# Another order of the scan directions, a layer norm finished half by half, and routing arithmetic with operands in PSUM

## The chip, the cores and the metric

The kernel runs as one program on one core of a Trainium2 chip. The metric is the device time of one execution in microseconds (us). Three timed executions of the kernel before took 4451.01, 4462.27 and 4446.85 us; their median is 4451.01 us. The profiled execution is a fourth one.

The core has five engines with a queue each, and each queue runs in order: TensorE (PE in the profile, its weight loads PEld), VectorE (DVE), ScalarE (ACT), GpSimd (POOL) and SyncE (SP), which here issues most of the transfers. SBUF and PSUM are the two on-chip memories; PSUM has eight banks of 128 x 512 fp32 values.

## The reference, cut to what matters

Four images of 384 channels x 32 x 32 pass through two layers. All is fp32.

```python
# layer 0
x = x + scan_conv(ln_channels(x, 1e-6))      # four scan directions, then layer norm and gelu
t = tokens(x)                                # [4, 1024, 384]
t = t + moe(ln_tokens(t, 1e-5))              # 4 experts, the best 2 of each token
# layer 1
x = x + attention(ln_channels(x, 1e-6))      # 8 heads over 1024 tokens
t = t + ffn(ln_tokens(t, 1e-5))              # weights are Kronecker products

def scan_conv(x):
    xs = [x, x.T, reversed(x), reversed(x.T)]        # k = 0..3: by rows, by columns, both again reversed
    for k: h = h * exp(dt * A) + dt * u * B;  y_k = sum_n(h * C) + u
    y = y_0 + y_2 + transpose back(y_1 + y_3)
    return gelu(ln_channels(y, 1e-5) * lnw + lnb)

def moe(t):
    p = softmax(t @ gate_w + gate_b); keep the two largest of four, divide by their sum + 1e-9
    return sum over the kept experts e of p_e * (gelu(t @ w1[e] + b1[e]) @ w2[e] + b2[e])
```

The sum of the four directions does not depend on the order in which they are added, apart from rounding.

## The kernel before, in words

**The scan** (`scan_layer`, lines 196 to 303). A *unit* is one image b, one direction k and one half i of the 1024 tokens (512 positions); the list `units` at lines 252 to 257 has 32 of them, eight to an image, in the order k = 0, 1, 2, 3. Directions 2 and 3 run backwards, so their second half comes first. Each unit has three channel chunks; `chunk` (line 401) makes for each of four groups g of states the products `bx` on POOL (L432, 128x1024), the decay `da` on ACT (L441, into PSUM), the recurrence on DVE (L446) and the product with C, half of it on POOL (L460) and half on DVE (L453). PE adds the states up into one PSUM bank `acc` (L467), and DVE adds `acc` to the output y (L294, L298). There are six buffers for `bx`, two for each group g, and each comes free when PE has read it at L467. In PSUM the scan has four banks: two for `da` and two under the tag "ps", which `acc`, the projections (`xd_ps`, `dt_ps`) and the layer norms (`ln_mean`, `ln_var`, `ln_rows`) share.

Beside a unit, `project` (line 305) prepares the next one. In the last unit of an image, `start` (line 223) loads the next image and norms both its halves first. After the last unit of an image `finish` (line 236) norms y (both halves, one after the other), applies gelu per chunk, adds the input on POOL (L247) and stores the result in DRAM as `x1[b]` (L248); then the tail of the image before it is emitted.

**The tail** of an image: `route` (line 611) with `spread` (line 616), which transposes the tokens of `x1[b]`, two blocks of 128 at a time, and computes gate scores; `places` (line 676), a chain of some 55 small DVE instructions that turns scores into row numbers, weights and expert numbers; then 16 indirect DMAs on POOL that scatter normed tokens into rows by expert (L664). `experts` (line 817) runs eleven slots of rows, `combine` (line 916) gathers the results, `prologue` (line 953) norms, `attention` (line 974) and `last_layers` (line 1077) follow. `less_mean` (line 540) is one DVE instruction of 128x8 used by `spread` and, through `prologue` and L958, by the attention: the ACT work at L960 waits for it. `divide` (line 1026) inverts the softmax sums (L1028).

**What sets the order.** A scheduler orders the instructions of each engine ahead of time from their program order (earlier is preferred), priorities (`high_priority` around `route`, `combine`, `prologue` and `last_layers`) and its own estimate of time. So the tail of image b-1 and the routing of image b run between the scan instructions of image b+1, in a fixed order per engine. During the scan the tail has four PSUM banks: two under the tag "s" (one tile), one "o" (expert outputs `y_ps`, attention `o_acc`, `f_acc` of the last layer) and one "p" (most else). When the scan is over, the tail of image 3 gets rooms of its own in what the scan leaves.

Of the kernel before, what the change touches and what calls it, by code (L numbers as in the profile page):

```python
# [9 lines left out]
F32 = mybir.dt.float32  # L10
# [16 lines left out]
KG = 4  # L27
NS = 16
# [86 lines left out]
class Body:  # L115
# [80 lines left out]
    def scan_layer(self, x1, between):  # L196

        nc, tc, a = self.nc, self.tc, self.a
        with ExitStack() as ctx:
# [36 lines left out]
            def finish(b, y):  # L236
                self.layernorm(y, y, self.eps5, psum, work)
                for c in range(DC):
                    ins = nc.scalar.activation(
                        y[:, c, :], y[:, c, :], AF.Gelu,  # L240
                        bias=self.col("lnb", c), scale=self.col("lnw", c),
                    ).ins
                    rows = slice(c * P, (c + 1) * P)
                    for i in range(NH):
                        x = work.tile([P, HF], F32, tag="k2", name="x", bufs=6)
                        nc.sync.dma_start(out=x, in_=a["x"][b][rows, halves(i)])
                        nc.gpsimd.tensor_add(x, x, y[:, c, halves(i)])  # L247
                        nc.sync.dma_start(out=x1[b][rows, halves(i)], in_=x)  # L248
                self.exp_again(ins)

# [4 lines left out]
                for k in range(KG)  # L255
# [10 lines left out]
            for n, unit in enumerate(units):  # L266
                b, k, i = unit
                fed, ahead = ahead, []
                project = iter(())
                if n + 1 < len(units):  # L270
                    nb = units[n + 1][0]
                    if nb not in us:
                        us[nb] = start(nb)
                    project = self.project(units[n + 1], us[nb], wx, work, dram, psum, ahead)
                    next(project)
                if n % NH == 0:
                    carry = wp.tile([P, NB * NG], F32, tag=f"carry{n // NH % 2}", name="carry")
                if k == 0 and i == 0:
                    y = work.tile([P, DC, L], F32, tag="y", name="y")
                for c in range(DC):  # L280
                    acc = psum.tile([P, HF], F32, tag="ps", name="acc")
                    for _ in self.chunk(
                        unit, n % NH == 0, c, fed, carry, nega, sel, acc, work, dap
                    ):
                        next(project, None)
                    if k % 2 == 0:
                        ys = y[:, c, halves(i)]
                        out = acc
                    else:
                        w = slice(i * (HW // NH), (i + 1) * (HW // NH))  # L290
                        ys = y[:, c, :].rearrange("p (h w) -> p h w", h=HW)[:, :, w]
                        out = acc.rearrange("p (w h) -> p h w", h=HW)
                    if k == 0:
                        nc.vector.scalar_tensor_tensor(  # L294
                            ys, us[b][:, c, halves(i)], dsum[:, c : c + 1], out, op0=ALU.mult, op1=ALU.add
                        )
                    else:
                        nc.vector.tensor_add(ys, ys, out)  # L298
                if k == KG - 1 and b not in self.under_way:
                    self.under_way[b] = fed[2]  # L300
                if n + 1 == len(units) or units[n + 1][0] != b:
                    finish(b, y)
                    between(b)
# [236 lines left out]
    def less_mean(self, mean, rstd, room, tag):  # L540

        less = room.tile([P, MB], tag, "less")
        self.nc.vector.scalar_tensor_tensor(less, mean, -1.0, rstd, op0=ALU.mult, op1=ALU.mult)
        return less
# [71 lines left out]
    def spread(self, b, x1, room):  # L616
# [10 lines left out]
        for m in range(0, MB, 2):  # L627
            x = room.tile([P, DC, 2 * P], "k4", "x")
            nc.sync.dma_start(out=x, in_=src[:, :, m * P : (m + 2) * P])
            xt = room.tile([P, 2, D], "k4", "xt")  # L630
            for o in range(2):
                ps = room.bank("p", "tt_ps")
                cols = slice(o * P, (o + 1) * P)
                for c in range(DC):
                    nc.tensor.transpose(ps[:, c * P : (c + 1) * P], x[:, c, cols], self.ident)
                for c in range(DC):
                    nc.tensor.matmul(
                        ps[:, D : D + NE], x[:, c, cols], self.wg[:, c, :],
                        start=(c == 0), stop=(c == DC - 1),
                    )  # L640
                nc.scalar.copy(xt[:, o, :], ps[:, :D])
                nc.vector.tensor_copy(sc[:, m + o, :], ps[:, D : D + NE])
                nc.vector.bn_stats(st[:, m + o, :], xt[:, o, :])
                nc.vector.bn_aggr(mv[:, m + o, :], st[:, m + o, :])
# [31 lines left out]
    def places(self, sc, room):  # L676
# [4 lines left out]

        def over(v):
            return v.unsqueeze(2).to_broadcast([P, nt, NE])

        red = room.tile([P, nt], "g_red", "g_red")
# [4 lines left out]
        nc.vector.reciprocal(red, red)  # L690
        nc.vector.tensor_mul(sc, sc, over(red))
# [3 lines left out]
        other = sc.unsqueeze(2).to_broadcast(shape)  # L695
        above = room.tile(shape, "g_above", "g_above")
        same = room.tile(shape, "g_same", "g_same")
# [5 lines left out]
        nc.vector.tensor_reduce(rank, above, AX.X, ALU.add)  # L703
        chosen = room.tile([P, TOP, nt, NE], "g_chosen", "g_chosen")
        for k in range(TOP):
            nc.vector.tensor_scalar(chosen[:, k], rank, float(k), None, op0=ALU.is_equal)
        nc.vector.tensor_scalar(rank, rank, float(TOP), None, op0=ALU.is_lt)
        nc.vector.tensor_mul(sc, sc, rank)
        nc.vector.tensor_reduce(red, sc, AX.X, ALU.add)
        nc.vector.tensor_scalar_add(red, red, 1e-9)  # L710
        nc.vector.reciprocal(red, red)
        nc.vector.tensor_mul(sc, sc, over(red))
# [7 lines left out]
        cnt = room.tile([P, 2, nt, NE], "g_cnt", "g_cnt")  # L720
        nc.vector.tensor_copy(cnt.rearrange("p t m e -> p (t m e)"), ps[:, : 2 * n])
        run = room.tile([P, nt + 1, NE], "g_run", "g_run")
        nc.vector.memset(run[:, 0, :], 0.0)
        for m in range(nt):
            nc.vector.tensor_add(run[:, m + 1, :], run[:, m, :], cnt[:, 1, m, :])

# [3 lines left out]
            need, run[:, nt, :].unsqueeze(2).to_broadcast([P, NE, ns]),  # L730
# [3 lines left out]
        used = room.tile([P, 2, NE], "g_used", "g_used")  # L734
        nc.vector.tensor_reduce(used[:, 1], need, AX.X, ALU.add)
        nc.vector.tensor_reduce(used[:, 0], need[:, :, 1::2], AX.X, ALU.add)
        nc.vector.scalar_tensor_tensor(
            used[:, 1], used[:, 0], -2.0, used[:, 1], op0=ALU.mult, op1=ALU.add
# [12 lines left out]
        shift = room.tile([P, 2, NE], "g_shift", "g_shift")  # L751
        full, back = shift[:, 0], shift[:, 1]
# [24 lines left out]
        nc.vector.tensor_add(at, at, ends)  # L777
        pick = room.tile([P, 2, TOP, nt, NE], "g_pick", "g_pick")
        both = [P, TOP, nt, NE]
        nc.vector.tensor_mul(pick[:, 0], chosen, at.unsqueeze(1).to_broadcast(both))  # L780
        nc.vector.tensor_mul(pick[:, 1], chosen, sc.unsqueeze(1).to_broadcast(both))
        picked = room.tile([P, 2, TOP, nt], "g_picked", "g_picked")
# [32 lines left out]
        return pos, picked[:, 1], expert  # L815
# [158 lines left out]
    def attention(self, xc, sums, room):  # L974
# [51 lines left out]
        def divide(t, att):  # L1026
            inv = room.tile([P, 2 * MB], "inv", "inv")
            nc.vector.tensor_add(inv, sums[:, t, :, 0], sums[:, t, :, 1])  # L1028
# [387 lines left out]
```

## Time and profile before

| quantity | value |
|---|---|
| three timed executions | 4451.01, 4462.27, 4446.85 us, median 4451.01 us |
| profiled execution, its own time | 4452.07 us |
| its span (first to last instruction) | 4450.2 us, so 1.9 us lie around it |
| mean granted TensorE clock | 0.850 |
| units of image 0 (from the first `bx` of one to that of the next) | 83.1 to 95.8 us |
| shortest and longest unit of images 1 to 3 | 97.5 us and 147.1 us |
| first `bx` product of images 0, 1, 2, 3 | at 47.8, 748.8, 1668.6, 2631.6 us |
| last addition of `acc` to y (end of the scan) | at 3569.1 us |
| first transpose of image 3's experts | at 3691.6 us |

How to read it: a timeline line has the start and the length in us, engine, line of the kernel, operation, out<-in, and how many instructions are merged; in brackets stands how long the engine was idle before, and what ended that. A group line has count, busy us and mean ns of one instruction, then the idle time before the group. A line of the 40 slices has one digit for each fortieth of the span (111 us): the busy share in tenths.

### The profile page before, as it was taken

The numbers are of one execution on the slowest core, as the hardware profiler recorded it, in microseconds if no ns is written. First come the engines' busy times: TensorE is split into PE (matmuls) and PEld (weight loads), VectorE is DVE, ScalarE is ACT, GpSimd is POOL, SyncE is SP. The second block draws the span as 40 slices with busy tenths as digits, with TensorE's granted clock in tenths as the row PEclk, the third lists the DMA queues.
The fourth block names the chain that finished last, engine by engine and source line by source line (L and its number), as shares of the span: only waits on it lengthen the run. The fifth ranks groups of instructions, "written<-read, shape, count | busy, mean of one in ns | idle before, by whom it ended". The sixth has DMA issues, their size and how long they took to land. (4 is left out here: it accounts for less than half of the span.)

```text
span 4450.2 us, 47090 instructions
## 1 busy us (share of the span) xinstructions
PE 3462.1 (78%) x13980; PEld 1644.5 (37%) x13980; DVE 2980.1 (67%) x4252; ACT 2469.7 (55%) x4380; POOL 3050.0 (69%) x1475
## 2 busy tenths in 40 slices
PE   6545554579995887669998688758998699999897
PEld 2111111245552222325555222214555334566333
DVE  5889998778887876978787777988787720020002
ACT  4545554456664766466666477466666453325354
POOL 4999999689988877779888689879888710000100
PEclk7766665579997998679999899869999899999898
DMA  4444453468785533357779434446778534344300
GB/s 121 119 124 114 129 162 91 134 225 233 217 253 169 164 93 116 117 174 217 209 229 274 134 99 120 123 145 193 215 212 261 171 106 139 123 135 164 102 17 15
DMA packets 404760, 684.81 MB, mean 154 GB/s; under 512 B 50960, under 2 KB 206480, under 8 KB 404496
## 3 DMA queue, kind: packets, MB, share of 16 engines
q1 hardware_dynamic: 395184, 655.37, 50.0%
q0 software_dynamic: 8192, 25.17, 1.7%
q8 instruction: 112, 1.84, 0.2%
q14 instruction: 152, 1.25, 0.1%
q10 hardware_dynamic: 1120, 1.18, 0.1%
HBM read 561.47 MB, written 120.06 MB: 153 GB/s over the span
## 5 line engine op out<-in xcount | busy, mean ns | idle before, releaser
L432 POOL TENSOR_TENSOR bx<-dtr,bcs 128x1024 f32<-128x1024 f32 x768 | 1793.5, 2362 | 211.5 <-PE acc L467 118.2
L441 ACT ACTIVATE da<-dtr,nega 128x512 f32<-128x512 f32 x1536 | 1045.8, 691 | 1013.9 <-DVE bx L453 637.7
L460 POOL TENSOR_TENSOR bx<-bx,bcs 128x1024 f32<-128x1024 f32 x384 | 904.0, 2360 | 216.9 <-DVE bx L446 94.9
L467 PE MATMUL acc<-bx,sel 128*32 128x512 f32 x3072 | 518.6, 712 | 304.2 <-POOL bx L460 258.4
L889 PE MATMUL h_ps<-xc,w 128*128 128x256 f32 (+1 forms) x3168 | 665.2, 364 | 43.6 <-DVE xc L871 21.1
L905 PE MATMUL y_ps<-w,hs 128*128 128x384 f32 x1824 | 644.1, 505 | 44.3 <-ACT hs L898 40.3
L889 PEld LDWEIGHTS h_ps<-xc,w 128*128 128x128 f32 x3168 | 547.4, 196 | 228.6 <-issue 92.0
L446 DVE TENSOR_TENSOR_SCAN bx<-da,carry,bx 128x512 f32<-128x512 f32 x384 | 473.9, 1269 | 125.1 <-ACT da L441 61.9
L446 DVE TENSOR_TENSOR_SCAN da<-da,carry,bx 128x512 f32<-128x512 f32 x384 | 477.3, 1273 | 70.6 <-ACT da L441 61.3
L446 DVE TENSOR_TENSOR_SCAN bx<-da,bx 128x512 f32<-128x512 f32 x384 | 451.8, 1209 | 102.6 <-POOL bx L432 61.3
L453 DVE TENSOR_TENSOR bx<-da,bcs 128x512 f32<-128x512 f32 x768 | 511.3, 680 | 4.5
L446 DVE TENSOR_TENSOR_SCAN da<-da,bx 128x512 f32<-128x512 f32 x384 | 455.7, 1219 | 74.5 <-ACT da L441 62.9
L905 PEld LDWEIGHTS y_ps<-w,hs 128*128 128x128 f32 x1824 | 348.6, 196 | 339.6 <-issue 78.2
L1020 ACT ACTIVATE ex<-s_ps 128x512 f32<-128x512 f32 x512 | 299.2, 590 | 207.1 <-PE s_ps L1015 206.1
L1015 PE MATMUL s_ps<-w 64*128 64x512 f32 x1024 | 307.6, 675 | 83.0 <-ACT ex L1020 83.0
L467 PEld LDWEIGHTS acc<-bx,sel 128*32 128x32 f32 x3072 | 78.6, 116 | 606.1 <-POOL bx L460 371.0
L1064 PE MATMUL o_acc<-ex,vt 128*64 128x512 f32 x1024 | 295.3, 657 | 0.6 <-ACT att L1072 0.5
L894 ACT ACTIVATE hs<-h_ps,bb 128x256 f32<-128x256 f32 (+1 forms) x528 | 193.6, 449 | 148.5 <-PE h_ps L889 148.3
L1105 POOL TENSOR_TENSOR xt<-xt,wb 128x3072 f32<-128x3072 f32 x4 | 26.7, 6686 | 310.4 <-DMA wb<-in_wb 310.4
L909 DVE TENSOR_TENSOR y<-y_ps,bb 128x384 f32<-128x384 f32 x76 | 41.6, 548 | 244.0 <-PE y_ps L905 244.0
L926 POOL TENSOR_TENSOR diag<-ident,g_picked 128x1024 f32<-128x1024 f32 x8 | 15.0, 1895 | 243.1 <-PE xc_ps L868 223.8
L1015 PEld LDWEIGHTS s_ps<-w 64*128 64x128 f32 x1024 | 80.9, 192 | 257.6 <-ACT ex L1020 153.4
(215 smaller groups left out, 4026.3 us busy)
## 6 DMA issues: line engine op xcount, KB each, us to landing
w<-in_w SPq DMA_DIRECT2D x352, 576.0 KB
dtr<-dd SPq DMA_DIRECT2D x1536, 128.0 KB
bcs<-rows SPq DMA_DIRECT2D x512, 128.0 KB
dd<-one_e SPq DMA_DIRECT2D x96, 256.0 KB
dd<-mag SPq DMA_DIRECT2D x96, 256.0 KB
rows<-zero SPq DMA_DIRECT2D x76, 192.0 KB
xs<-rows SPq DMA_DIRECT2D x32, 384.0 KB
made<-y SPq DMA_DIRECT2D x32, 384.0 KB
```

The costliest lines, as they stand in the source:

```text
L432: pool = nc.gpsimd.tensor_mul(bx, dtr[q][1], bc[:, 0].unsqueeze(1).to_broadcast([P, 2, HF])).ins
L441: nc.scalar.activation(da, dtr[q][0][:, j, :], AF.Exp, scale=nega[:, col : col + 1])
L446: nc.vector.tensor_tensor_scan(run(h), run(da), run(bx[:, j, :]), 0.0 if first else hold, ALU.mult, ALU.add,)
L453: dve = nc.vector.tensor_mul(bx[:, j, :], h, cg).ins
L460: pool = nc.gpsimd.tensor_mul(bx, bx, cg.unsqueeze(1).to_broadcast([P, 2, HF])).ins
L467: nc.tensor.matmul(acc[lo : lo + DB, :], sel, out[q][:, j, :], start=(g == 0), stop=(g == NG - 1),)
L889: nc.tensor.matmul(ps[:, r, :], w1[(f + r) // wf][:, c, (f + r) % wf * P : ((f + r) % wf + 1) * P], xc[:, c, :], start=(c == 0), stop=(c = ...
L894: nc.scalar.activation(hs[:, f + r, :], ps[:, r, :], AF.Identity, bias=bb[:, f + r : f + r + 1])
L905: nc.tensor.matmul(out[:, :D], hs[:, f, t * P : (t + 1) * P], w2[f // wf][:, f % wf, :], start=(f == 0), stop=(f == FC - 1),)
L1015: nc.tensor.matmul(ps[:, o, :], w[rows, j * P : (j + 1) * P], w[rows, halves(i)], start=True, stop=True,)
L1020: ins = nc.scalar.activation(ex[:, o, :], ps[:, o, :], AF.Exp, scale=HD**-0.5, accum_out=sums[:, t, 2 * j + o, i : i + 1],).ins
L1064: ins = nc.tensor.matmul(out[cols, :], made[t][1][:, j, cols], ex[:, o, :], start=(j == 0), stop=(j == MB - 1),).ins
```

## The change

1. The directions of an image run in the order 0, 1, 3, 2. The last two units are then direction 2 (rows, backwards): its unit with the second half of the tokens, then that with the first half.
2. `finish` takes one half. It is called after each of these two units, so the second half of the tokens is normed, given its gelu, added to the input and stored during the last unit. Gelu runs on 512 columns instead of 1024 and twice as often; so do the loads of its function table. For images 0 to 2 the next image's `start` runs in that same last unit.
3. `spread` takes the second half of the tokens first. For image 0 it uses a two-bank "s" tile for a pair of blocks, and copies both at once.
4. `places` keeps about half of its small tiles in one PSUM bank, taken from tag "o", so that its two-operand DVE instructions have at least one operand there. Some values exist twice (`prob` beside `sc`, `blocks`, `total`, `weight`).
5. `less_mean` has ACT copy `rstd` to PSUM (tag "p") first; `divide` sums with one `tensor_reduce` instead of adding two slices.

```diff
+ORDER = (0, 1, 3, 2)
...
-            def finish(b, y):
-                self.layernorm(y, y, self.eps5, psum, work)
+            def finish(b, y, i):
+
+                self.layernorm(y, y, self.eps5, psum, work, parts=[i])
                 for c in range(DC):
                     ins = nc.scalar.activation(
-                        y[:, c, :], y[:, c, :], AF.Gelu,
+                        y[:, c, halves(i)], y[:, c, halves(i)], AF.Gelu,
                         bias=self.col("lnb", c), scale=self.col("lnw", c),
                     ).ins
                     rows = slice(c * P, (c + 1) * P)
-                    for i in range(NH):
-                        x = work.tile([P, HF], F32, tag="k2", name="x", bufs=6)
...
-                for k in range(KG)
+                for k in ORDER
...
-                if k == KG - 1 and b not in self.under_way:
-                    self.under_way[b] = fed[2]
-                if n + 1 == len(units) or units[n + 1][0] != b:
-                    finish(b, y)
-                    between(b)
+                if k == ORDER[-1]:
+                    self.under_way.setdefault(b, fed[2])
+                    finish(b, y, i)
+                    if n + 1 == len(units) or units[n + 1][0] != b:
+                        between(b)
...
         less = room.tile([P, MB], tag, "less")
-        self.nc.vector.scalar_tensor_tensor(less, mean, -1.0, rstd, op0=ALU.mult, op1=ALU.mult)
+        ps = room.bank("p", "less_ps")[:, :MB]
+        self.nc.scalar.copy(ps, rstd)
+        self.nc.vector.scalar_tensor_tensor(less, mean, -1.0, ps, op0=ALU.mult, op1=ALU.mult)
...
-        for m in range(0, MB, 2):
+        for m in [*range(MB // 2, MB, 2), *range(0, MB // 2, 2)]:
...
+            both = room.two("tt_ps") if b == 0 else None
...
+        area = room.bank("o", "places")
...
-        red = room.tile([P, nt], "g_red", "g_red")
+        red, prob = small([P, nt]), small([P, nt, NE])
...
+        nc.vector.tensor_mul(prob, sc, over(red))
         nc.vector.tensor_mul(sc, sc, over(red))
...
-        other = sc.unsqueeze(2).to_broadcast(shape)
+        other = prob.unsqueeze(2).to_broadcast(shape)
         above = room.tile(shape, "g_above", "g_above")
-        same = room.tile(shape, "g_same", "g_same")
+        same = small(shape)
...
-        cnt = room.tile([P, 2, nt, NE], "g_cnt", "g_cnt")
+        cnt = small([P, 2, nt, NE])
...
-        used = room.tile([P, 2, NE], "g_used", "g_used")
+        used = small([P, 2, NE])
...
+        weight = room.tile([P, TOP, nt], "g_weight", "g_weight")
+        nc.vector.tensor_copy(weight, picked[:, 1])
+        return pos, weight, expert
...
-            nc.vector.tensor_add(inv, sums[:, t, :, 0], sums[:, t, :, 1])
+            nc.vector.tensor_reduce(inv, sums[:, t], AX.X, ALU.add)
```

`small(shape)` cuts the next free columns from `area`.

## The prediction

> **What bounds the kernel now.** I read first the slices and the busy times, then the scan unit by unit, then the stall times of small DVE instructions, then the stretch behind the scan. From the page, in this order: the span; the slices of DVE and of POOL; and the costliest group, whose last part is the idle time before it.
>
> ```profile
> span 4450.2 us, 47090 instructions
> ...
> DVE  5889998778887876978787777988787720020002
> ...
> POOL 4999999689988877779888689879888710000100
> ...
> L432 POOL TENSOR_TENSOR bx<-dtr,bcs 128x1024 f32<-128x1024 f32 x768 | 1793.5, 2362 | 211.5 <-PE acc L467 118.2
> ```
>
> POOL is full (9) only in image 0; from slice 7 on, where tails run beside the scan, it has 6 to 9, and DVE nearly the same. From slice 32 on both are idle: there PE works alone. So the scan's length decides to 3569 us, PE behind it. A unit needs 24 x 2.362 + 12 x 2.360 us = 85.0 us of POOL's products. Units of image 0 take 83.1 to 95.8 us, those of images 1 to 3 97.5 to 147.1. In the windows of the three longest, DVE is busy 112.3 of 141.0, 122.9 of 147.1 and 123.1 of 141.1 us, and POOL idles 36 to 38 us in each. PE has more to spare there (87 us). DVE's time and DVE's waits make units long.
>
> Some of that time is no work. Groups of DVE by line and form (count, busy us, mean ns of one):
>
> ```profile
> L543 DVE SCALAR_TENSOR_TENSOR less<-mv,rstd 128x8 f32<-128x8 f32 x8 | 35.9, 4485 | 1.8 <-ACT rstd L151 1.8
> L1028 DVE TENSOR_TENSOR inv<-sums 128x16 f32<-128x16 f32 x16 | 18.6, 1163 | 179.6 <-ACT ex L1020 179.6
> L687 DVE TENSOR_TENSOR sc<-sc,g_red 128x32 f32<-128x32 f32 x4 | 4.5, 1132 | 0.1
> L909 DVE TENSOR_TENSOR y<-y_ps,bb 128x384 f32<-128x384 f32 x76 | 41.6, 548 | 244.0 <-PE y_ps L905 244.0
> L1098 DVE TENSOR_TENSOR wc<-wc,cols 128x384 f32<-128x384 f32 x4 | 3.9, 965 | 5.2 <-DMA wc<-in_wc 5.2
> ```
>
> An addition of 128x16 takes 1163 ns where one of 128x384 with an operand in PSUM takes 548: size doesn't explain it. The timeline around one `less` (start, length, merged count; idle before in brackets):
>
> ```profile
> 1425.90 4.63 POOL L432 TENSOR_TENSOR bx<-dtr,bcs 128x1024 f32<-128x1024 f32 x2
> ...
> 1426.00 12.68 DVE L543 SCALAR_TENSOR_TENSOR less<-mv,rstd 128x8 f32<-128x8 f32 x1 [0.61 <-ACT rstd L151]
> 1430.51 1.25 POOL L388 TENSOR_TENSOR lnw<-lnw,mag 128x512 f32<-128x512 f32 x1
> 1431.73 6.92 POOL L432 TENSOR_TENSOR bx<-dtr,bcs 128x1024 f32<-128x1024 f32 x3
> 1438.60 2.44 DVE L446 TENSOR_TENSOR_SCAN bx<-da,carry,bx 128x512 f32<-128x512 f32 x2
> 1438.76 4.89 ACT L960 ACTIVATE got<-xt,less,rstd 128x384 f32<-128x384 f32 x8 [12.79 <-DVE less L543]
> 1441.19 2.35 POOL L460 TENSOR_TENSOR bx<-bx,bcs 128x1024 f32<-128x1024 f32 x1 [2.54 <-DVE bx L446]
> ```
>
> The `less` of eight columns begins with POOL's run of six products and ends with it, at 1438.65. I read it so: a DVE instruction with two SBUF operands doesn't get in while POOL has products back to back. The recurrences behind it then start late, and POOL pays: 2.54 us idle here, 8.48 before its next product. The other two long ones (11.63 us at 2485.5, 10.80 at 3536.3) look alike; the remaining five take 0.16 each.
>
> [...]
>
> **The change, part by part**, each as what the end gains (+) or loses (-).
>
> *Places.* Lines 686 to 814 keep DVE busy 26.7, 23.3 and 25.9 us in the three routes under the scan, and 11.0 in the fourth behind it, where POOL is still: 15.7 + 12.3 + 14.9 = 42.9 us of stalls. POOL idles 59 us in the stretches of the three (845 to 896, 1861 to 1918, 2919 to 2971). In the new code two-operand instructions have one operand in PSUM, so the stalls should go. Not all comes back: what is late next is `bx` by its six buffers and `da` by ACT. I take **+35**, bounds +20 (half) and +43.
>
> *Less.* 35.9 - 8 x 0.16 = 34.6 us of stalls; POOL idle right behind them 28.6 us (2.54 + 8.48, 5.44 + 3.85, 8.29). The third lies in the last unit, where less follows. The ACT copy of `rstd` adds a hop of 0.2 to 0.6 us by the wait of 0.61 above, hidden by nothing in `prologue`. I take **+22**, bounds +10 and +35.
>
> *Divide.* A clean `inv` takes 0.18 us, so 18.6 - 16 x 0.18 = 15.8 us were stalls, 10.5 of them in one at 2817.36, behind which POOL idles 8.50. A one-input reduction isn't shown to stall (L783, 0.28 us for 128x128). **+10**, bounds +3 and +16.
>
> *PSUM operands and extra instructions.* Of L1098's four, one ran undisturbed: 0.50 us with both operands in SBUF, against L909's 0.548 with one in PSUM: 0.05 us more. For some 50 instructions in three routes that is 7 us, with the few copies in it: **-7**, bounds 0 and -12. [...]
>
> *Halves of the layer norm.* A half took 18.9, 14.0, 23.1, 16.7, 15.2, 15.7 us (y) and 18.9, 18.4, 13.4, 15.2, 19.5, 15.6 us (u, in the last units): mean h = 17.05. What they cost now shows on POOL. At an image's end both halves of y, one after the other, stand ahead of the x additions, and in the last unit both halves of u stand ahead of the first `acc`, because `xd_ps`, `ln_*` and `acc` share two banks:
>
> ```profile
> 1599.89 7.01 POOL L432 TENSOR_TENSOR bx<-dtr,bcs 128x1024 f32<-128x1024 f32 x3 [24.05 <-PE acc L467]
> ...
> 1719.12 7.44 POOL L247 TENSOR_TENSOR x<-x,y 128x512 f32<-128x512 f32 x6 [22.54 <-ACT y L239]
> ```
>
> Such gaps sum to 7.5 + 24.05 + 20.52 = 52.1 us in the three last units and 16.22 + 22.54 + 19.51 = 58.3 at the three transitions. Six halves at 17.05 are 102.3, so what POOL still had in hand (products for the `bx` buffers, additions) covers 102.3 - 52.1 = 50.2 in the one place, 102.3 - 58.3 = 44.0 in the other. In the changed order of the engines one half of y stands ahead of both halves of u in the last unit, and all three ahead of the first `acc`; the transition keeps one half. With today's covers the gaps become 9h - 50.2 and 3h - 44.0, together 12h - 94.2, against 110.4 now: a loss of 12h - 204.6. That is **0** at h = 17.05: three halves wait in another place, and no fewer. Bounds: h = 14, near the shortest rows, gives 36.6 back, some **+35** as a transition's gap can't fall below nothing; h = 20.4, as much above the mean, **-40**. Gelu's ACT work in halves lies beside other halves and is in neither.
>
> *At nothing:* the order of the directions (the same loads and products; it only lets the last two units be by rows), the order of blocks in `spread`, and the paired copies of image 0, where eight copies of ACT (L641, 476 ns) and eight of DVE (L642, 150 ns) become four of each. All lie beside the scan; without that cover they are worth under 3 us.
>
> *Behind the scan.* One half of y is left there instead of two. Now:
>
> ```profile
> 3612.24 0.37 SPq L629 DMA_DIRECT2D x<-x  x1
> ...
> 3661.99 1.03 POOL L664 DMA_INDIRECT rows<-xt,g_pos  x1 [50.60 <-DVE g_pos L788]
> ...
> 3691.60 1.54 PE L868 MATMUL xc_ps<-ident,xs 128*128 128x128 f32 x6 [6.04 <-DMA xs<-rows]
> ```
>
> The token load leaves 43.1 us behind the scan, the first scatter 92.9, the first expert transpose 122.5. With one half fewer each comes 17 to 25 us earlier. But PE isn't waiting for it: from 3564.6 to 3691.6 it idles 16.8 us in all, since attention(2) runs there, and from 3692 to 4050 it is busy 358 of 358. By the changed order 22 attention steps, not 30, stand ahead of the first transpose; 8 x 2.14 us (PE's time for a step there, two of L1015 and two of L1064) = 17 us move behind it and must be done anyway. So what remains is some 6.5 us of PE work for one half norm, now done under the scan,, and part of the idle: **+10**, bounds -10 (order worse packed around 4146 to 4190, where PE idles 19 us) and +25. On SP the second half's loads and stores are issued in the last unit, ahead of the tail's; `spread` of image 3 reads only after SP has issued the first half's stores, so it doesn't start earlier than that.
>
> Sum: 35 + 22 + 10 - 7 + 0 + 10 = **70 us**. Own time 4452.07 - 70 = 4382; the profiled execution is 1 us above the median, so **4381**. Less than 0.3%, 13 us, can't be told from no change.
>
> **The rivals.**
>
> 1. *DVE's time isn't the limit.* When it comes free, ACT's `da` or PE's clock (0.58 to 0.68 in those units) takes its place, and PE's in-order tail matmuls delay `acc`. For it: POOL waits mostly for `acc` (118.2 us). Against: the gaps follow directly on the stalls. The three stall terms halve (67 to 33), so the sum is 36 and the time 4452 - 36 - 1 = 4415.
>
> 2. *Three halves in series decide; slower.* The first `acc` waits for them, and halves beside each other get longer. Its place is the two shared banks in the last units of images 0 to 2; its price 12 us for each us of h over 17.05. For it: halves of 23.1 and 19.5 exist, and a half beside a start runs on the same ACT and PE. Against: the mean. The other terms sum to 70, so it is slower from h = 17.05 + 70 / 12 = 22.9, and by more than 13 us from 24.0. At h = 26 it gives 4451 + 12 x 3.1 = 4488.
>
> 3. *Everything comes back.* All stall terms at their upper bounds and h = 14: 43 + 35 + 16 - 7 + 35 + 10 = 132; 4452 - 132 - 1 = 4319.
>
> 4. *The change doesn't do what it says.* `places` now holds the bank of tag "o" for its whole chain, and `f_acc` of the last layers wants it: at 1908.1 before `g_pos` at 1917.8, at 2955.5 before 2971. Matmuls queued behind `f_acc` on PE, `acc` among them, would wait up to 10 + 16 = 26 us. With rival 1's 36, less 26, and nothing (instead of +10) behind the scan, the sum is 0: 4451, no change.
>
> **Chances.** Forecast .55 (own range 4340 to 4420), rival 1 .16, rival 3 .11, rival 4 .07, rival 2 .11. Range 4310 to 4440: it holds the first three. Faster .82, same .07, slower .11.
>
> **What the profile after would show.** `less` at 0.2 us eight times; `places` busy 11 to 14 us in all four routes; `inv` near 0.3; units (1,0), (2,1), (3,2) in the order of time below 125 us; no gap over 10 us ahead of the x additions at a transition, but 28 to 36 us ahead of the first `acc` in last units (over 45 would be rival 2); the scan's end near 3510; the first expert transpose 100 to 106 us behind it. The prediction is wrong if PSUM operands stall too, if halves get longer beside each other, or if POOL's idle time stays and only changes its releaser.

## The result and the profile after

The changed kernel took 4400.43 us (median of four executions, 4396.59 to 4405.50) beside 4452.9 us of the kernel before (4446.85 to 4462.27). The ratio is 0.988, with a 95% interval of 0.9865 to 0.9895: 53 us faster, where 70 were forecast.

From the page of the changed kernel, the same lines as before (L432 is L434 now; the line numbers move by one or two here, by thirty behind `places`):

```profile
span 4394.8 us, 47123 instructions
...
DVE  5889996878866868968887677978787720002102
...
POOL 4999996889878969788998788878898810000100
...
L434 POOL TENSOR_TENSOR bx<-dtr,bcs 128x1024 f32<-128x1024 f32 x768 | 1793.7, 2360 | 237.4 <-PE acc L469 138.3
```

The last addition of `acc` to y starts at 3518.5 us instead of 3569.1: 50.6 of the 55.4 us between the two spans lie in the scan, 4.8 behind it. The shape is the old one: POOL full in image 0, 6 to 9 later, DVE alike.

The groups of DVE by line and form in the changed kernel (count, busy us, mean ns):

```profile
L658 DVE TENSOR_TENSOR sc<-sc,rstd 128x32 f32<-128x32 f32 x4 | 5.5, 1362 | 1.0 <-ACT rstd L152 1.0
L836 DVE TENSOR_TENSOR g_half<-g_ef,g_half 128x2 f32<-128x2 f32 x4 | 4.9, 1226 | 0.0
L1060 DVE TENSOR_REDUCE inv<-sums 128x16 f32<-128x32 f32 x16 | 2.9, 183 | 184.7 <-ACT ex L1052 184.7
L547 DVE SCALAR_TENSOR_TENSOR less<-mv,less_ps 128x8 f32<-128x8 f32 x8 | 1.3, 156 | 1.9 <-ACT less_ps L546 1.9
L715 DVE TENSOR_TENSOR places<-sc,places 128x32 f32<-128x32 f32 x4 | 0.7, 183 | 0.1
```

`less` went from 4485 to 156 ns in the mean, `inv` from 1163 to 183, L687 (L715 now) from 1132 to 183. L658 and L836 still have two SBUF operands, and wait (1362 and 1226 ns in the mean, 1032 and 164 before). The four `places` are busy 22.4, 11.9, 14.9 and 11.5 us instead of 26.7, 23.3, 25.9 and 11.0; the first has 12.2 us left in six instructions that work on SBUF alone (at L788, L824, L836, L839 and L840).

The timeline of the changed kernel around the `less` that took 12.68 us:

```profile
1403.89 4.66 POOL L462 TENSOR_TENSOR bx<-bx,bcs 128x1024 f32<-128x1024 f32 x2
...
1408.51 6.97 POOL L434 TENSOR_TENSOR bx<-dtr,bcs 128x1024 f32<-128x1024 f32 x3
1408.59 0.17 ACT L546 COPY less_ps<-rstd 128x8 f32<-128x8 f32 x1
1408.79 0.16 DVE L547 SCALAR_TENSOR_TENSOR less<-mv,less_ps 128x8 f32<-128x8 f32 x1 [0.24 <-ACT less_ps L546]
1409.03 4.89 ACT L992 ACTIVATE got<-xt,less,rstd 128x384 f32<-128x384 f32 x8 [0.28 <-DVE less L547]
```

It starts 0.28 us into a run of POOL and is done while the first product of that run goes on. The hop over ACT costs some 0.2 us: DVE's wait of 0.24 us holds the copy's 0.17.

The POOL timeline around the last unit of image 1, changed kernel (start, length; in brackets how long POOL was idle before, and what ended it):

```profile
1590.98 3.74 POOL L248 TENSOR_TENSOR x<-x,y 128x512 f32<-128x512 f32 x3 [7.40 <-ACT y L241]
1625.71 13.93 POOL L434 TENSOR_TENSOR bx<-dtr,bcs 128x1024 f32<-128x1024 f32 x6 [30.99 <-PE acc L469]
```

Three halves in series make a gap of 31 us ahead of the first `acc`; the other two last units have 28.4 and 32.9. The gaps of 16 to 23 us ahead of the x additions at the transitions are gone: of the six gaps there now (two to an image, one of them in the last unit) none is over 8.05 us.

Behind the scan, changed kernel:

```profile
3536.77 0.38 SPq L633 DMA_DIRECT2D x<-x  x1
...
3586.96 1.03 POOL L675 DMA_INDIRECT rows<-xt,g_pos  x1 [50.63 <-DVE g_weight L846]
...
3615.45 1.54 PE L900 MATMUL xc_ps<-ident,xs 128*128 128x128 f32 x6 [9.70 <-DMA xs<-rows]
```

The token load leaves 18.3 us behind the scan (43.1 before), the first scatter 68.5 (92.9), the first expert transpose 97.0 (122.5). Each is some 25 us earlier, and the stretch is only 4.8 us shorter.

One wait of rival 4 is there too. The PE timeline of the changed kernel in the second unit of image 2:

```profile
1844.43 2.04 PE L469 MATMUL acc<-bx,sel 128*32 128x512 f32 x8
1860.22 2.78 PE L1197 MATMUL f_acc<-hs,wc 128*32 128x512 f32 x10 [13.75 <-DVE g_weight L846]
```

`f_acc` starts 0.15 us after the last instruction of `places`, which gives the bank back, and PE stood idle for 13.75 us; in image 3 it waits 8.14 us in the same way. POOL's own gaps in that stretch are 3.52 us and less: its buffers cover most of it.

### The profile page after: what moved, and what is told of

It is laid out like the page before. It is cut to its first block, busy times and chain, and to the rows that moved or that the text cites. A ratio compares the mean times of both kernels' runs of the same rounds, so it can differ in the third digit from the quotient of the medians.

```text
span 4394.8 us, 47123 instructions
## 1 busy us (share of the span) xinstructions
PE 3448.4 (78%) x13980; PEld 1647.6 (37%) x13980; DVE 2901.9 (66%) x4256; ACT 2479.0 (56%) x4402; POOL 3050.7 (69%) x1475
## 4 chain that ended last, share of the span: by engine, by line
PE 39%; DVE 23%; ACT 11%; POOL 9%; DMA 9%; issue 7%; SPq 2%; DVEq 0%; POOLq 0%; ACTq 0%
PE y_ps L937 8%; PE h_ps L921 8%; DVE da L448 8%; DVE bx L448 8%; POOL bx L434 4%; PE s_ps L1047 4%; DMA dtr<-dd 4%; PE o_acc L1096 4%; ACT da L443 3%; PE acc L469 3%; DVE bx L455 3%; POOL bx L462 2%; PE xd_ps L332 2%; DMA w<-in_w 2%; PE w_ps L1024 1%
## 5 line engine op out<-in xcount | busy, mean ns | idle before, releaser
L434 POOL TENSOR_TENSOR bx<-dtr,bcs 128x1024 f32<-128x1024 f32 x768 | 1793.7, 2360 | 237.4 <-PE acc L469 138.3
L359 PE MATMUL dt_ps<-xd,wdt 12*128 12x512 f32 x192 | 123.7, 729 | 53.6 <-ACT mag L398 27.4
```

What stands on the lines that cost most here:

```text
L434: pool = nc.gpsimd.tensor_mul(bx, dtr[q][1], bc[:, 0].unsqueeze(1).to_broadcast([P, 2, HF])).ins
```

## The experiments

Twelve kernels ran. The runs stood in three groups, each with runs of the kernel before beside it: 4475.5, 4454.2 and 4476.3 us in the median. So times are compared by ratio to the kernel before of the same group; 0.1% is 4.5 us.

### Each part alone, and an unexpected sign

**e1_places** has the new `places` and nothing else, **e4_halves** `ORDER`, `finish` by halves and the new `spread`, as the diff of the change shows them. **e2_less** and **e3_divide** in full:

```diff
-        self.nc.vector.scalar_tensor_tensor(less, mean, -1.0, rstd, op0=ALU.mult, op1=ALU.mult)
+        ps = room.bank("p", "less_ps")[:, :MB]
+        self.nc.scalar.copy(ps, rstd)
+        self.nc.vector.scalar_tensor_tensor(less, mean, -1.0, ps, op0=ALU.mult, op1=ALU.mult)
```

```diff
-            nc.vector.tensor_add(inv, sums[:, t, :, 0], sums[:, t, :, 1])
+            nc.vector.tensor_reduce(inv, sums[:, t], AX.X, ALU.add)
```

> The kernel before with the new places alone. Theory (its two-operand instructions no longer wait for POOL, and the scan gets most of that time back): 35 less 6 for PSUM operands, so 29 us faster (15 to 40), with places busy 11 to 15 us in all four routes. Rival (DVE's time is not the limit): at most 12 us faster, with POOL idle as much as before in the units where places runs. Rival (the bank of tag o is held too long): f_acc later than g_pos and no gain.

> The kernel before with less_mean alone changed: ACT copies rstd to PSUM first. Theory: the three long waits (12.7, 11.6, 10.8 us) become 0.16 us each, 22 us faster (10 to 35). Rival (the long waits hide in time that is lost anyway): under 8 us faster, though the waits are gone.

> The kernel before with divide alone changed: one tensor_reduce of 128x32 in SBUF instead of an addition of two SBUF slices. Theory: a reduction does not wait for POOL; 16 of them take 0.2 us each instead of 1.16, and the kernel gains 10 us (3 to 16). Rival (every DVE instruction on SBUF waits): the mean stays near 1 us and the time within 5 us of before.

> The kernel before with the order 0, 1, 3, 2, finish by halves and the new spread, but places, less_mean and divide as before. Theory from the gaps on POOL of the changed kernel (92.4 us ahead of the first acc in three last units and 21 ahead of the x additions, against 52.1 and 58.3 before): the scan gains nothing, behind it some 5 us; 5 us faster (-10 to +15). Rival (three halves in a row cost more than the transitions give): 15 to 30 us slower, and then the three other edits gained 67 to 82 together. Rival (the restructure carries the change): over 20 us faster.

Measured, as ratio to before: e1_places 1.0063 (1.0045 to 1.0082), e2_less 1.0086 (1.0072 to 1.0100), e3_divide 1.0043 (1.0030 to 1.0056), e4_halves 1.0073 (1.0056 to 1.0091). All four are **slower**, by 28, 38, 19 and 33 us. The waits were gone all the same in two of them: `less` took 158 ns in e2_less, `inv` 182 in e3_divide. In e1_places the three routes under the scan still took 15.7, 23.9 and 14.9 us, and `f_acc` waited 8.47 us for the bank, as its last rival says, but that is no loss of 28. In e4_halves the loss of 33 us is close to its first rival (15 to 30, and the three other edits worth 67 to 82). For `less` and `divide` neither the theory nor a rival fits, and the parts don't add up to the whole.

What else differs is the order. The scheduler orders the instructions of all engines from its own estimate of time, so a changed line gives another order from that place on, on every engine. In e3_divide, where one instruction is exchanged for another in each of 16 places, PE's matmuls stand in the order of before for the first 7584 of 13980 rows of the trace, and in another one from there on.

### The same edits with the order held

To take that away, the kernels of the next runs carry a list of the order that the scheduler gave the kernel before (or the changed one), and tie each instruction to the one ahead of it on its engine. This is an edge of order only, without a wait:

```python
def hold(tc, nc):
    ...
    for engine, text in HELD.items():
        step = np.frombuffer(zlib.decompress(base64.b85decode(text)), np.int16).astype(int)
        last = None
        for at in np.cumsum(step + 1) - 1:
            ins = traced[engine][at]
            if last is not None:
                tc.add_manual_dep(ins, last.name, same, reason="held order")
            last = ins
```

**h1_less** and **h2_divide** are e2_less and e3_divide at the order of the kernel before.

> less_mean alone again, but with every engine's instructions held in the order of the kernel before (the eight ACT copies put in right behind the instruction they read). Theory (the waits for POOL cost time, and the loss of the run without the held order came from the order that the scheduler made anew): 22 us faster than before (10 to 35). Rival (the PSUM bank or the ACT hop costs more than the waits): slower by 10 to 36, as without the held order. Rival (the waits hide in lost time): within 8 us.

> divide alone again, with the order of the kernel before held on every engine. Theory: 10 us faster (3 to 16), so the order made anew cost some 31 us in the run without the hold. Rival (the reduction itself costs): slower, by up to 21.

Measured: h1_less 0.992 (0.9905 to 0.9936), 36 us faster, as against 38 slower with an order made anew: the same program in another order is 74 us apart. h2_divide 0.9993 (0.9983 to 1.0004): 3 us, within what can be told from nothing, as against 19 slower. No run holds an order and changes nothing else; h2_divide, which comes nearest to it, ends within 8 us of the kernel before.

The timeline of h1_less where the kernel before had its wait of 12.68 us:

```profile
1420.07 4.67 POOL L432 TENSOR_TENSOR bx<-dtr,bcs 128x1024 f32<-128x1024 f32 x2
...
1420.18 0.17 ACT L544 COPY less_ps<-rstd 128x8 f32<-128x8 f32 x1
1420.38 0.16 DVE L545 SCALAR_TENSOR_TENSOR less<-mv,less_ps 128x8 f32<-128x8 f32 x1 [0.81 <-ACT less_ps L544]
```

POOL starts a run at 1420.07, `less` gets through at 1420.38. 36 us (28 to 42) is as much as the 34.6 us of the waits, and not the 22 that the prediction took.

For `divide` the longest wait shows why so little came. `wc` (L1098) is a product of two SBUF operands, `inv_rows` (L1033) a copy that waits its turn behind it on DVE, and L1040 stands ahead of `acc` on PE. The kernel before:

```profile
2817.36 10.53 DVE L1028 TENSOR_TENSOR inv<-sums 128x16 f32<-128x16 f32 x1 [0.98 <-ACT ex L1020]
...
2828.10 0.50 DVE L1098 TENSOR_TENSOR wc<-wc,cols 128x384 f32<-128x384 f32 x1
...
2832.38 1.97 PE L1040 MATMUL bc_ps<-inv_rows,ident 16*64 16x128 f32 x16 [3.54 <-DVE inv_rows L1033]
...
2836.36 4.66 POOL L432 TENSOR_TENSOR bx<-dtr,bcs 128x1024 f32<-128x1024 f32 x2 [8.50 <-PE acc L467]
```

and h2_divide, the same place:

```profile
2820.53 0.19 DVE L1028 TENSOR_REDUCE inv<-sums 128x16 f32<-128x32 f32 x1 [0.93 <-ACT ex L1020]
...
2824.75 6.75 DVE L1098 TENSOR_TENSOR wc<-wc,cols 128x384 f32<-128x384 f32 x1 [3.74 <-PE inv_ps L1031]
...
2835.29 1.97 PE L1040 MATMUL bc_ps<-inv_rows,ident 16*64 16x128 f32 x16 [10.64 <-DVE inv_rows L1033]
...
2839.27 4.66 POOL L432 TENSOR_TENSOR bx<-dtr,bcs 128x1024 f32<-128x1024 f32 x2 [8.20 <-PE acc L467]
```

`inv` no longer waits, but the next instruction with two SBUF operands does: `wc` takes 6.75 us instead of 0.50, until POOL's run is over. In both kernels `inv_rows` comes behind that wait, L1040 behind `inv_rows`, and `acc` behind L1040; so POOL's gap of 8.50 us is still 8.20. In the whole kernel `inv` lost 15.7 us and `wc` gained 5.2 of them. This run has put one wait in the place of another: that the gap comes from the wait, as the prediction has it, is not refuted by that.

**h3_back** is the changed kernel at its own order, with the operands back in SBUF:

```diff
-        area = room.bank("o", "places")
+        area = room.tile([P, 376], "g_area", "g_area")
...
-        ps = room.bank("p", "less_ps")[:, :MB]
+        ps = room.tile([P, MB], tag + "_s", "less_s")
...
-            nc.vector.tensor_reduce(inv, sums[:, t], AX.X, ALU.add)
+            nc.vector.tensor_add(inv, sums[:, t, :, 0], sums[:, t, :, 1])
```

> The changed kernel at its own order, held on every engine, but with the operands back in SBUF: the area of places, the copy of rstd, and divide as an addition of two slices. Theory (the waits carry the gain): it gives back 45 to 65 us and ends within 15 us of the kernel before. Rival (the new order carries it, the waits hide): it keeps 35 us or more of the 52. In between, each has its share.

Measured: 1.0057 (1.0042 to 1.0072), so 79 us slower than the changed kernel (1.0057 / 0.988 = 1.0179; some 9 us either way by the two intervals) and 25 slower than before. The theory had the right cause and too small a size; that the new order carries the gain is refuted. The groups of DVE in h3_back:

```profile
L547 DVE SCALAR_TENSOR_TENSOR less<-mv,less_s 128x8 f32<-128x8 f32 x8 | 38.7, 4833 | 2.0 <-ACT less_s L546 1.9
L1060 DVE TENSOR_TENSOR inv<-sums 128x16 f32<-128x16 f32 x16 | 18.6, 1164 | 185.3 <-ACT ex L1052 185.3
L715 DVE TENSOR_TENSOR g_area<-sc,g_area 128x32 f32<-128x32 f32 x4 | 3.5, 864 | 0.1
```

With the order held and the operands in the other memory, the same instructions wait again: 38.7 us for eight of `less`, against 35.9 in the kernel before.

**h4_places_back** has only the first of the three edits above, at the same held order.

> The changed kernel at its own order, held, with the area of places alone back in SBUF (less_mean and divide stay changed). Theory (the parts add up: three edits gave 79 us at this order, less 36 and divide 3 at the order of before): places is worth some 40 us, so this ends 8 to 17 us faster than the kernel before. Rival (the waits overlap and one edit gets what another leaves): places alone gives back under 20 us, and this ends 30 to 50 us faster than before.

Measured: 0.9975 (0.9962 to 0.9988), 42 us slower than the changed kernel (0.9975 / 0.988 = 1.0096). In it the three `places` under the scan are busy 29.4, 26.3 and 28.2 us as against 22.4, 11.9 and 14.9: 34.7 us of DVE time, and 42 us of the end. `less` and `divide` are then worth 1.0057 - 0.9975 = 0.82%, 37 us, at the changed order, and 36 + 3 were measured at the order of before: with an order held, the parts agree. The other half of this test, the new `places` at the order of the kernel before, wasn't tried: there the bank of tag "o" is needed by other tiles while `places` would hold it.

### The order of the directions

**o1_directions** changes one thing in the kernel before:

```diff
+ORDER = (0, 1, 3, 2)
...
-                for k in range(KG)
+                for k in ORDER
```

> The kernel before with the directions in the order 0, 1, 3, 2 and nothing else; the order of the instructions on every engine comes out the same, one for one. Theory (the directions cost nothing): within 8 us of before. Rival (the 27 us that the middle units lose when finish goes by halves come from the directions): 20 to 30 us slower, with middle units (the third to the seventh of images 1 to 3) 20 to 30 us longer in sum.

Measured: 1.0020 (1.0009 to 1.0031), 9 us slower with the instructions in the same order one for one. That is just over the bound of 8 us, and not the 20 to 30 us of the rival. The prediction had it at nothing. The middle units take 1654.0 us in sum here, against 1639.9 in p1_operands, a run of the same group in the order of before (one execution each), so the loss seems to lie there. How the directions cost it isn't shown.

### Three edits without the halves

**s1_three**: `places`, `less_mean` and `divide` as in the changed kernel, all else as before, the order made anew.

> places, less_mean and divide changed, finish and the directions as before; the order is made anew. Theory (the three edits are worth 79 us, finish by halves costs 26): 79 us faster than before, and faster than the changed kernel, if the order made anew costs nothing; the three edits alone cost 24 to 72 us by their orders, so 10 to 80 us faster. Rival (the three edits only pay together with the halves): no faster than before.

Measured: 1.0029 (1.0018 to 1.0041), 13 us slower, as the rival says. By the theory the order made anew would have cost 92 us here, more than in any pair measured. A part of it can be seen. Busy time of each engine from the end of the scan to the end of the span (length; busy us and instructions of PE, PEld, DVE, ACT, POOL; clock, DMA share, GB/s), o1_directions and then s1_three, which were of one group:

```profile
3594.00:4484.80 890.80, 815.54 (x3475) 416.90 (x3473) 111.56 (x279) 392.04 (x832) 55.18 (x42) 0.94 0.30 100
```

```profile
3575.20:4493.40 918.20, 835.29 (x3519) 428.89 (x3519) 112.44 (x282) 400.00 (x849) 55.20 (x42) 0.94 0.31 100
```

s1_three leaves 44 matmuls more for the time behind the scan, 20 us of PE work, and the stretch is 27 us longer. In e2_less and e3_divide it is 913.0 and 917.8 us. So some of the tail's work that lay under the scan in the order of before lies behind it in these. The rest, in the scan itself, isn't settled: that the three edits pay less without the halves remains possible.

### The halves apart

**a1_apart** takes the three halves of the last unit apart, the order made anew:

```diff
                 for c in range(DC):
+                    if c == 2 and rest is not None:
+                        self.layernorm(us[rest], us[rest], self.eps6, psum, work, parts=[1])
+                        rest = None
+                    if c == 1 and half is not None:
+                        finish(*half)
+                        half = None
                     acc = psum.tile([P, HF], F32, tag="ps", name="acc")
```

> The changed kernel with the three halves of layer norm in the last unit apart: half 0 of u ahead of the unit, half 1 of y behind its first chunk, half 1 of u behind its second. Theory (each half alone is covered by what POOL has in hand, 15 to 17 us): the gaps ahead of the first acc fall from 31 to under 5 us each and the kernel is 60 to 90 us faster than the changed one, 110 to 140 faster than before. Rival (the halves delay the later chunks as much as they delayed the first): within 20 us of the changed kernel, with the gaps moved behind the first chunk. The order is made anew here, which by the first four runs may cost or give some 30 us.

Measured: 0.9995 (0.9983 to 1.0007), as slow as the kernel before and 51 us slower than the changed one. The POOL timeline of a1_apart, the same last unit of image 1:

```profile
1591.87 13.93 POOL L445 TENSOR_TENSOR bx<-dtr,bcs 128x1024 f32<-128x1024 f32 x6 [17.05 <-PE acc L480]
1628.42 1.27 POOL L400 TENSOR_TENSOR mag<-one_e,mag 128x512 f32<-128x512 f32 x1 [6.27 <-ACT one_e L387]
1649.87 4.71 POOL L445 TENSOR_TENSOR bx<-dtr,bcs 128x1024 f32<-128x1024 f32 x2 [18.84 <-PE acc L480]
```

One half alone makes a gap of 17 to 19 us here (9 to 24 over the three last units), not under 5; over these three units POOL idles 132.9 us, as against 115.1 in the changed kernel. The theory falls: the cover is not to be had again for each half. Three last units are 25 us longer in sum; how much of the other 26 is the order isn't settled.

### Which instructions wait

**p1_operands** puts one small DVE instruction, of six kinds in turn, behind 18 chunks of image 0 in the kernel before:

```diff
+                        if j % 6 == 0:
+                            nc.vector.tensor_add(pr, pa[:, :, 0], pa[:, :, 1])
+                        elif j % 6 == 1:
+                            nc.vector.tensor_add(pr, acc[:, :8], pa[:, :, 1])
+                        elif j % 6 == 2:
+                            nc.vector.tensor_reduce(pr, pa, AX.X, ALU.add)
+                        elif j % 6 == 3:
+                            nc.vector.tensor_scalar(pr, pa[:, :, 0], 2.0, None, op0=ALU.mult)
...
```

> The kernel before with one small extra DVE instruction of 128x8 behind each of 18 chunks of image 0, where POOL is never idle; six kinds in turn, three of each: an addition of two SBUF operands, one with an operand in PSUM, a reduction, a multiplication by a constant, a copy and a reciprocal, the last four on SBUF alone. Theory (an operand in PSUM, or an instruction with one read, does not wait for POOL): the first takes 2 to 13 us, the second, third and sixth under 0.4 us; multiplication and copy are open (the trace of before has a copy of 128x16 at 642 ns in the mean, L788). Rival (every DVE instruction on SBUF alone waits): all but the second take over 1 us.

The groups of p1_operands:

```profile
L312 DVE TENSOR_SCALAR pr<-pa 128x8 f32<-128x8 f32 x3 | 8.1, 2711 | 0.1
L314 DVE COPY pr<-pa 128x8 f32<-128x8 f32 x3 | 4.8, 1611 | 0.0
L306 DVE TENSOR_TENSOR pr<-pa 128x8 f32<-128x8 f32 x3 | 3.2, 1055 | 0.1
L316 DVE RECIPROCAL pr<-pa 128x8 f32<-128x8 f32 x3 | 0.6, 189 | 0.0
L310 DVE TENSOR_REDUCE pr<-pa 128x8 f32<-128x16 f32 x3 | 0.5, 163 | 0.1
L308 DVE TENSOR_TENSOR pr<-acc,pa 128x8 f32<-128x8 f32 x3 | 0.5, 156 | 0.0
```

An operand in PSUM (L308), a reduction and a reciprocal never took over 0.21 us. The addition of two SBUF operands took 0.97 and 2.03 us (its third ran ahead of the scan, in 0.17), the copy up to 2.33, the multiplication up to 7.22. (One copy and one reciprocal ran while POOL was idle.) So one operand fewer isn't the rule: a copy and a multiplication by a constant waited with a single operand (2.33 and 7.22 us).

How long they wait shows in the timeline of p1_operands:

```profile
210.98 11.59 POOL L450 TENSOR_TENSOR bx<-dtr,bcs 128x1024 f32<-128x1024 f32 x5
...
213.32 2.33 DVE L314 COPY pr<-pa 128x8 f32<-128x8 f32 x1
...
560.50 7.22 DVE L312 TENSOR_SCALAR pr<-pa 128x8 f32<-128x8 f32 x1
560.72 2.34 POOL L478 TENSOR_TENSOR bx<-bx,bcs 128x1024 f32<-128x1024 f32 x1
563.01 4.68 POOL L450 TENSOR_TENSOR bx<-dtr,bcs 128x1024 f32<-128x1024 f32 x2
```

The copy is over at 215.65, with the second of five products (215.62), and the other three follow without a pause. The multiplication, begun at 560.50 while an earlier product ran, is over at 567.72, behind three more, the last of which ended at 567.69; then POOL was idle for 2.81 us. The kernel before has both kinds: of its DVE instructions of at most 128 columns, 40 took over 0.6 us and ended with an instruction of POOL. 36 of them waited for no more than one, 2.43 us at most, and in 25 of these POOL went on without a pause. The other four (three of `less`, one of `inv`) waited through five or six, until POOL fell idle. Which of the two it will be, no run here shows.

## Why the prediction was right, and where it wasn't

The sign, the cause and the range held; 17 us of the 70 didn't come, by errors of both signs.

- **The reading of the waits** held for the three long ones, but not as a rule. "A DVE instruction with two SBUF operands doesn't get in while POOL has products back to back": 36 of 40 waits in the same trace ended with one instruction of POOL. The sums went by the rows, so they don't suffer by it.
- **Less** was taken at +22 and gave 36 at a held order. The step "POOL idle right behind them 28.6 us" looked for the price in POOL's gaps; the whole of DVE's lost time was the price.
- **Places** with its PSUM operands was taken at 35 - 7 = 28 and gave 42, although the first route kept its waits. "What is late next is `bx` by its six buffers and `da` by ACT" failed: nothing took the place of the waits. The new wait for bank "o" is in this number already. The price of the PSUM operands, 7 us, was too high, too: in the fourth route, where POOL is still, `places` takes 11.5 us with them and 11.4 without (h4_places_back).
- **Divide** was taken at +10 and gave 3 (-2 to +8). The step took all 15.8 us of `inv` for lost time that ends; at the largest of its waits `wc` waited instead, and 5.2 us came back there. Why the rest paid so little isn't shown.
- Together 79 us (h3_back against the changed kernel) where 60 were summed. Rival 1, that DVE's time isn't the limit, is refuted by h1_less and h3_back.
- **Halves** at 0: that number couldn't come out otherwise, because the covers are worked out from the gaps with the same mean h that then gives the new gaps. Ahead of `acc` 28.4, 31.0 and 32.9 us came, as forecast (28 to 36). By place, the sum has 103.3 us ahead of `acc` and 7.1 ahead of the x additions; measured are 92.4 and 30.4, so 122.8 against 110.4 before. Yet with the waits kept (h3_back), the last units and the two behind each add up to 1139.7 us, against 1140.3 in the kernel before. Rival 2's sign, a gap over 45 us, didn't come.
- **What the sum lacked** is 25 us that the rest of the change costs in h3_back against before. 9 of it are the directions, put "at nothing" because loads and products are the same. By units, in executions that lie 33 us apart, h3_back loses 27 us in the third to seventh units of images 1 to 3 (1662.9 against 1635.6), where no half is normed, and 9 us in the last unit of all, which now holds a half that stood behind the scan. For the first no term existed. The directions have a part in it (14 us in o1_directions, by one execution); that the rest is another order of the tail's work beside the scan isn't shown.
- **The order made anew** had no term either, and here luck helped. It stands in the 25 us above; by the same kind of sum it cost 22 us in e3_divide, 74 in e2_less and 92 in s1_three. With 92 in place of the 25, the changed kernel would have been no faster than before.
- **Behind the scan**, +10 became 5: everything starts 25 us earlier, and PE has the same work to do, as the step said.
- Of the signs to look for, `less`, `inv`, the transitions, the gaps ahead of `acc` and the scan's end (3518 for 3510) came as told. Units (1,0), (2,1) and (3,2) were to be below 125 us and took 132.9, 126.4 and 137.7 us; `places` was to take 11 to 14 us and took 22.4 and 14.9 in two routes; the first expert transpose came 97.0 us behind the scan, not 100 to 106.
- Two readings of the prediction are off and move nothing: its "three longest" units leave out unit (2,0) with 145.9 us, and the 7.5 us of image 0 are no gap ahead of `acc` in the trace (POOL idles 5.67 us for DVE and 2.57 for `acc` in that unit).

So 79 - 25 = 54, as measured (a sum that closes by its making, as both terms are read from h3_back). The halves pay nothing by themselves (e4_halves 1.0073 and h3_back 1.0057, two orders of nearly the same work, agree), and at a held order the operands in PSUM carry the change. There DVE's busy time on the pages goes with the time: 35.8 us less in h1_less, 81.0 less in the changed kernel than in h3_back, for 36 and 79 us. In s1_three, with an order made anew, it is 73.5 us less than before, and the time is 13 us more.

## What to carry to other kernels

A DVE instruction of a few columns that took microseconds was waiting here (`less` of 128x8: 12.68 us at most, 0.16 undisturbed). Set such a time beside POOL's run of instructions, and try an operand in PSUM (`less` then took 0.16 us in the mean of eight) or a form that didn't wait here (`inv` as a reduction, 0.18 us in the mean of 16). Where a scheduler makes the order, one part of a change measured alone measures its new order too (74 us between two orders of one program here): hold the order, and only then compare. Before a wait is counted as gained, look at what stands behind it on the same engine: the next instruction of the same kind may take the wait over, as `wc` did from `inv` (6.75 us in h2_divide, 0.50 in the kernel before).

## What was not expected of the hardware

- A small DVE instruction that waited while POOL worked mostly did so for the one instruction that POOL had under way (36 of 40 in the kernel before, 2.43 us at most), but some were held through a whole run until POOL fell idle: 12.68 us over six instructions there, 7.22 us over three and the end of a fourth in p1_operands.
- In p1_operands single-operand copy and multiplication in SBUF waited likewise (2.33 and 7.22 us at most); reduction and reciprocal didn't (0.15 to 0.20 us).
